# Relational graph layer: message table and per-edge gathers replaced by gathers of h, sums by (type, node) in a ring, and a transform behind a branch on TensorE

## The chip, the cores and the metric

One core of one Trainium2 chip. The metric is the device time of the whole kernel in microseconds (us), lower is better. A profile of one execution goes with each kernel. PE is TensorE, PEld its weight loads, PEq its sequencer, DVE VectorE, ACT ScalarE, POOL GpSimd, SP SyncE.

## The reference

```python
def _rgcn_layer(x, W, self_w, b, src, dst, edge_type, num_nodes):
    xW = jnp.einsum('ni,rio->rno', x, W)           # R = 8 relations, 256 x 256 each
    msg = xW[edge_type, src]                       # 320000 edges
    agg = jax.ops.segment_sum(msg, dst, num_segments=num_nodes)   # 20000 nodes
    return agg + x @ self_w + b

h = jnp.maximum(_layernorm(x, axis=-1), 0.0)
out = x + layer2(relu(layer1(h)))                  # two such layers, other weights (shortened)
```

The edges are sorted by dst, and dst is drawn so that low node numbers have many edges: the blocks of 128 nodes fill slowly at first and fast at the end.

## The kernel before

Each layer has two stages. The node phase multiplies every node by all eight matrices and writes a table of 164 MB; the edge phase gathers one row of that table per edge, 128 edges (a chunk) at a time, multiplies by a one-hot matrix and adds into an accumulator in SBUF.

```python
# node phase, per 128 nodes (cut)
for c in range(0, R * D, step):                                   # step = 512
    po = pp.tile([P, step], F32, name="po", bufs=4)
    for k in range(KD):
        nc.tensor.matmul(po[:n], lhsT=ht[:, k, :n], rhs=wf[:, k, c:c + step],
                         start=(k == 0), stop=(k == KD - 1))
    ...                                                           # copies to stage
nc.sync.dma_start(table[i * P:i * P + n].rearrange("n r o -> n (r o)"), stage[:n])

# edge phase (cut)
with tc.For_i(0, n, 1):                                           # 21 turns of 128 items a layer
    ...
    for u in range(GI):
        if u % OB == 0:
            hot = eb.tile([P, OB, P], F32, name="hot")
            nc.vector.tensor_tensor(hot, iota_f..., rel..., op=ALU.is_equal)
        msg = eb.tile([P, D], F32, name="msg", bufs=12)
        nc.gpsimd.indirect_dma_start(out=msg, ..., in_=table.rearrange("n r o -> (n r) o"), ...)
        pm = pp.tile([P, D], F32, name="pm", bufs=5)
        nc.tensor.matmul(pm, lhsT=hot[:, u % OB, :], rhs=msg, start=True, stop=True)
        a = agg[:, ds(ws[u % OB], 1), :].rearrange("p w d -> p (w d)")
        nc.vector.tensor_tensor(a, a, pm, op=ALU.add)
```

Of the kernel before, what the change touches and what calls it, by code (L numbers as in the profile page):

```python
"""Two-layer relational GNN block: out = x + rgcn2(relu(rgcn1(relu(layernorm(x))))).

Per layer:
  node phase   table[n, r] = h[n] @ W[r] for every node and relation (in DRAM), and
               agg[n] = h[n] @ self_w + b (+ x in layer 2), which stays in SBUF.
  edge phase   agg[dst] += table[src, type].  Edges are taken 128 at a time (a chunk); the
               nodes are cut into windows of 128.  One item is a (chunk, window) pair: the
               chunk's 128 messages are gathered and multiplied by the one-hot matrix of
               their places in the window.  A chunk gets an item for each window from its
               lowest to its highest dst, so any order of the edges is right; with edges  # L10
               sorted by dst there is little more than one item per chunk.
"""
# [9 lines left out]
F32 = mybir.dt.float32  # L22
I32 = mybir.dt.int32
BF16 = mybir.dt.bfloat16
AF = mybir.ActivationFunctionType
# [4 lines left out]
DVE = mybir.EngineType.DVE  # L30
P = 128
EPS = 1e-5


@with_exitstack
def gnn_kernel(ctx: ExitStack, tc: tile.TileContext, x, src, dst, etype, w1, sw1, b1, w2, sw2, b2, out):
# [4 lines left out]
    KD = D // P  # L41
    NW = (N + P - 1) // P
# [4 lines left out]
    REC = 2 * P + 1  # L47
    GI = 128
    OB = 8
    assert E % P == 0 and D % P == 0  # L50

    dram = ctx.enter_context(tc.tile_pool(name="dram", bufs=1, space=DRAM))
    table = dram.tile([N, R, D], F32, name="table")
    rec = dram.tile([C, REC], F32, name="rec")
    ends = dram.tile([1, C], F32, name="ends")

# [3 lines left out]
    iota_f = const.tile([P, P], F32, name="iota_f")  # L60
    nc.gpsimd.iota(iota_f, pattern=[[1, P]], base=0, channel_multiplier=0, allow_small_or_imprecise_dtypes=True)
    iota_p = const.tile([P, 1], F32, name="iota_p")
    nc.gpsimd.iota(iota_p, pattern=[[0, 1]], base=0, channel_multiplier=1, allow_small_or_imprecise_dtypes=True)
    eps_t = const.tile([P, 1], F32, name="eps_t")
    nc.vector.memset(eps_t, EPS)
    ngroups = const.tile([1, 1], I32, name="ngroups")

# [1 line left out]
    with tc.tile_pool(name="setup", bufs=1) as sp, tc.tile_pool(name="setup_ps", bufs=1, space=PSUM) as spp:  # L69
        src_i = sp.tile([CP, CA, P], I32, name="src_i")  # L70
        dst_i = sp.tile([CP, CA, P], I32, name="dst_i")
        typ_i = sp.tile([CP, CA, P], I32, name="typ_i")
        nc.sync.dma_start(dst_i, dst.rearrange("(p a e) -> p a e", p=CP, e=P))
        nc.scalar.dma_start(src_i, src.rearrange("(p a e) -> p a e", p=CP, e=P))
        nc.sync.dma_start(typ_i, etype.rearrange("(p a e) -> p a e", p=CP, e=P))

        rows = sp.tile([CP, CA, REC], F32, name="rows")
        nc.vector.scalar_tensor_tensor(rows[:, :, :P], src_i, float(R), typ_i, op0=ALU.mult, op1=ALU.add)
        nc.scalar.copy(rows[:, :, P:2 * P], dst_i)

        win = sp.tile([CP, 2, CA], I32, name="win")
        nc.vector.tensor_reduce(win[:, 0, :], dst_i, AX.X, ALU.min)
        nc.vector.tensor_reduce(win[:, 1, :], dst_i, AX.X, ALU.max)
        nc.vector.tensor_single_scalar(win, win, 7, ALU.arith_shift_right)
        winf = sp.tile([CP, 2, CA], F32, name="winf")
        nc.vector.tensor_copy(winf, win)
        cnt = sp.tile([CP, CA], F32, name="cnt")
        nc.vector.scalar_tensor_tensor(cnt, winf[:, 1, :], 1.0, winf[:, 0, :], op0=ALU.add, op1=ALU.subtract)
        zero = sp.tile([CP, CA], F32, name="zero")
        nc.vector.memset(zero, 0.0)  # L90
        end = sp.tile([CP, CA], F32, name="end")
        nc.vector.tensor_tensor_scan(end, cnt, zero, 0.0, ALU.add, ALU.add)
        before = sp.tile([CP, CP], F32, name="before")
        nc.vector.tensor_scalar(before, iota_f[:CP, :CP], iota_p[:CP], None, op0=ALU.is_gt)
        pre = spp.tile([CP, 1], F32, name="pre")
        nc.tensor.matmul(pre, lhsT=before, rhs=end[:, CA - 1:CA], start=True, stop=True)
        pre_s = sp.tile([CP, 1], F32, name="pre_s")
        nc.vector.tensor_copy(pre_s, pre)
        nc.vector.tensor_scalar(end, end, pre_s, None, op0=ALU.add)
        q = sp.tile([CP, CA], F32, name="q")  # L100
        nc.vector.tensor_tensor(q, end, cnt, op=ALU.subtract)
        nc.vector.tensor_tensor(rows[:, :, 2 * P], q, winf[:, 0, :], op=ALU.subtract)
        nc.sync.dma_start(rec.rearrange("(p a) r -> p a r", p=CP), rows)
        nc.scalar.dma_start(ends.rearrange("o (p a) -> (o p) a", p=CP), end)

        last = sp.tile([1, 1], F32, name="last")
        nc.sync.dma_start(last, ends[:, C - 1:C])
        last_i = sp.tile([1, 1], I32, name="last_i")
        nc.vector.tensor_scalar(last_i, last, float(GI - 1), None, op0=ALU.add)
        nc.vector.tensor_single_scalar(ngroups, last_i, 7, ALU.arith_shift_right)  # L110

    acc = ctx.enter_context(tc.tile_pool(name="acc", bufs=1))
    agg = acc.tile([P, NW, D], F32, name="agg")
    if TAIL < P:
        nc.vector.memset(agg[:, NW - 1, :], 0.0)

    def node_phase(layer, w, sw, b):
        with tc.tile_pool(name=f"na{layer}", bufs=1) as wp, tc.tile_pool(name=f"nb{layer}", bufs=2) as np_, \
                tc.tile_pool(name=f"np{layer}", bufs=2, space=PSUM) as pp:
            wt = wp.tile([P, KD, R + 1, D], F32, name="wt")  # L120
            for k in range(KD):
                nc.sync.dma_start(wt[:, k, :R, :], w[:, k * P:(k + 1) * P, :].rearrange("r i o -> i r o"))
                nc.scalar.dma_start(wt[:, k, R, :], sw[k * P:(k + 1) * P, :])
            bias = wp.tile([P, D], F32, name="bias")
            nc.scalar.dma_start(bias, b.partition_broadcast(P))
            wf = wt.rearrange("p k r o -> p k (r o)")
            for i in range(NW):
                n = P if i < NW - 1 else TAIL
                xt = np_.tile([P, D], F32, name="xt", bufs=3)
                nc.scalar.dma_start(xt[:n], x[i * P:i * P + n, :])  # L130
                if layer == 1:
                    st = np_.tile([P, 6], F32, name="st")
                    nc.vector.bn_stats(st[:n], xt[:n])  # L133
                    mv = np_.tile([P, 2], F32, name="mv")
                    nc.vector.bn_aggr(mv[:n], st[:n])
                    rs = np_.tile([P, 1], F32, name="rs")
                    nc.scalar.activation(rs[:n], mv[:n, 1:2], AF.Sqrt, bias=eps_t[:n])
                    nc.vector.reciprocal(rs[:n], rs[:n])
                    h = np_.tile([P, D], F32, name="h")
                    nc.vector.tensor_scalar(h[:n], xt[:n], mv[:n, 0:1], rs[:n], op0=ALU.subtract, op1=ALU.mult)  # L140
                    base = bias
                else:
                    h = agg[:, i, :]
                    base = np_.tile([P, D], F32, name="base")
                    nc.gpsimd.tensor_tensor(base[:n], xt[:n], bias[:n], op=ALU.add)  # L145
                pt = pp.tile([P, KD, P], F32, name="pt")
                for k in range(KD):
                    nc.tensor.transpose(pt[:, k, :n], h[:n, k * P:(k + 1) * P], ident[:n, :n])  # L148
                ht = np_.tile([P, KD, P], F32, name="ht")
                nc.scalar.activation(ht[:, :, :n], pt[:, :, :n], AF.Relu)  # L150
                stage = np_.tile([P, R * D], F32, name="stage")
                step = 512
                for c in range(0, R * D, step):
                    po = pp.tile([P, step], F32, name="po", bufs=4)
                    for k in range(KD):
                        nc.tensor.matmul(po[:n], lhsT=ht[:, k, :n], rhs=wf[:, k, c:c + step],  # L156
                                         start=(k == 0), stop=(k == KD - 1))
# [11 lines left out]
    def edge_phase(layer):  # L169
        with tc.tile_pool(name=f"ea{layer}", bufs=1) as ep, tc.tile_pool(name=f"eb{layer}", bufs=2) as eb, \  # L170
# [50 lines left out]
            with tc.For_i(0, n, 1):  # L221
                for a, bb in zip(cur, nxt):
                    nc.scalar.copy(a, bb)  # L223
# [56 lines left out]
```

## Time and profile before

| | before |
|---|---|
| time, median of 4 runs | 10729.6 us (10723.5 to 10740.6) |
| span of the profiled run | 10803.4 us |
| POOL busy / TensorE busy / VectorE busy | 52% / 66% / 36% |
| mean granted TensorE clock | 0.736 |
| node phases / edge phases | 2660 us / 8081 us |

The prediction below shows the rows of slices, the stretches, the timeline of a stretch and the groups, so they are not repeated.

### The profile page before, as it was taken

How to read it: one execution, taken by the hardware profiler on the slowest of the kernel's cores; microseconds unless marked ns; L12 is line 12 of the kernel's file. 1: busy time of each engine (PE TensorE's matmuls, PEld its weight loads, DVE VectorE, ACT ScalarE, POOL GpSimd, SP SyncE). 2: the span in 40 equal slices, each digit the busy share in tenths (PEclk: the TensorE clock that was granted, in tenths of full speed). 3: DMA queues.
4: the chain of work that ended last, by engine and by line, in shares of the span. 5: the costliest groups of instructions: out<-in, count | busy, mean ns of one | idle time of the engine just before them, and what ended most of it. 6: DMA issues, size and time to landing. Idle time of an engine off the chain costs nothing. (4 is left out here: it accounts for less than half of the span.)

```text
span 10803.4 us, 75643 instructions
## 1 busy us (share of the span) xinstructions
PE 7136.2 (66%) x17794; PEld 3836.9 (36%) x17794; DVE 3904.0 (36%) x7989; ACT 579.4 (5%) x1360; POOL 5624.2 (52%) x5585
## 2 busy tenths in 40 slices
PE   7999955556555555555599998565555555555554
PEld 3444423333333333333244444333333333333332
DVE  3333333434433433334322222433434433333333
ACT  1222200000000000000011111000000000000000
POOL 0000067666666666766600001666766666666665
PEclk9999966666666666666699999666766666666666
DMA  4333323322222223323343333223323232232324
GB/s 145 144 142 144 142 88 90 89 89 89 88 88 87 88 88 89 89 84 89 89 149 142 143 145 131 88 87 89 90 86 90 85 90 88 88 89 87 89 88 143
DMA packets 376495, 1115.33 MB, mean 103 GB/s; under 512 B 97320, under 2 KB 162184, under 8 KB 335624
## 3 DMA queue, kind: packets, MB, share of 16 engines
q0 software_dynamic: 260160, 710.78, 22.3%
q1 hardware_dynamic: 59992, 349.84, 8.7%
q10 hardware_dynamic: 56228, 53.28, 1.5%
q8 instruction: 59, 0.97, 0.0%
q14 instruction: 56, 0.46, 0.0%
HBM read 762.77 MB, written 350.74 MB: 103 GB/s over the span
## 5 line engine op out<-in xcount | busy, mean ns | idle before, releaser
L237 POOL DMA_INDIRECT msg<-table,key x5376 | 5467.3, 1017 | 2534.1 <-issue 1197.0
L241 PE MATMUL pm<-msg,hot 128*128 128x256 f32 x10752 | 4578.8, 566 | 3033.0 <-DVE agg L243 1264.6
L241 PEld LDWEIGHTS pm<-msg,hot 128*128 128x128 f32 x10752 | 2565.0, 271 | 5010.4 <-DVE agg L243 2100.4
L243 DVE TENSOR_TENSOR agg<-agg,pm 128x256 f32 x5376 | 2259.6, 420 | 2324.9 <-PE pm L241 1191.6
L156 PE MATMUL po<-wt,ht 128*128 128x512 f32 x5024 | 2227.3, 596 | 58.9 <-ACT ht L150 49.2
L230 DVE TENSOR_TENSOR hot<-iota_f,rel 128x1024 f32<-128x1024 f32 x672 | 820.8, 1227 | 2192.7 <-remote 1493.4
L156 PEld LDWEIGHTS po<-wt,ht 128*128 128x128 f32 x5024 | 940.5, 190 | 1161.3 <-issue 1039.9
L161 DVE COPY stage<-po 128x512 f32<-128x512 f32 x628 | 433.5, 691 | 1522.1 <-PE po L156 1522.1
L191 POOL DMA_INDIRECT row<-rec,ti x44 | 41.9, 952 | 1400.9 <-DVE ti L189 1388.1
L145 POOL TENSOR_TENSOR base<-xt,bias 128x256 f32<-128x256 f32 (+1 forms) x157 | 114.0, 726 | 1176.3 <-DVE agg L166 1160.5
L159 ACT COPY stage<-po 128x512 f32<-128x512 f32 x628 | 367.1, 585 | 1526.5 <-PE po L156 1485.7
L223 ACT COPY key<-key_n 128x128 int32<-128x128 int32 x42 | 12.5, 298 | 6143.7 <-PEq L221 6142.7
L164 PE MATMUL ps<-wt,ht 128*128 128x256 f32 x1256 | 323.9, 381 | 5.3 <-DMA wt<-in_L_gnn_self_w_dram 5.3
L208 PE MATMUL pt<-ident,row 128*128 128x128 f32 x44 | 19.7, 447 | 459.4 <-DMA row<-rec,ti 431.9
L164 PEld LDWEIGHTS ps<-wt,ht 128*128 128x128 f32 x1256 | 238.9, 190 | 172.2 <-issue 155.1
L208 PEld LDWEIGHTS pt<-ident,row 128*128 128x128 f32 x44 | 8.0, 182 | 489.3 <-issue 489.3
L133 DVE BATCH_NORM_STATS2 st<-xt 128x6 f32<-128x256 f32 (+1 forms) x157 | 64.7, 412 | 263.0 <-DMA xt<-in_x_dram 263.0
L187 DVE TENSOR_SCALAR_CACHE_REDUCE hit<-endb,item 128x2500 bf16<-128x2500 f32 x44 | 124.0, 2817 | 59.1 <-PEq L221 44.8
L150 ACT ACTIVATE ht<-pt 128x256 f32<-128x256 f32 x314 | 103.6, 380 | 511.3 <-PE pt L148 354.3
L198 DVE TENSOR_TENSOR wv<-item,row 128x1 f32<-128x1 f32 x44 | 7.0, 160 | 329.5 <-DMA row<-rec,ti 329.5
L214 ACT CAST win_n<-pw 1x128 int32<-1x128 f32 x44 | 11.2, 254 | 1399.6 <-remote 912.3
L166 DVE TENSOR_TENSOR agg<-ps,base 128x256 f32<-128x256 f32 (+1 forms) x157 | 66.7, 425 | 48.8 <-PE ps L164 38.1
(54 smaller groups left out, 545.9 us busy)
## 6 DMA issues: line engine op xcount, KB each, us to landing
table<-stage SPq DMA_DIRECT2D x312, 1024.0 KB, 4.1
msg<-table,key POOLq DMA_INDIRECT x5376
xt<-in_x_dram ACTq DMA_DIRECT2D x312, 128.0 KB, 3.9
out_dram<-agg SPq DMA_DIRECT2D x6, 1664.0 KB, 19.6
out_dram<-agg ACTq DMA_DIRECT2D x6, 1664.0 KB, 28.3
wt<-in_L_gnn_W_dram SPq DMA_DIRECT2D x4, 1024.0 KB, 15.4
rec<-rows SPq DMA_DIRECT2D x1, 2509.8 KB
endb<-ends SPq DMA_DIRECT2D x2, 1250.0 KB
```

The lines of the kernel that those rows point to most:

```text
L145: nc.gpsimd.tensor_tensor(base[:n], xt[:n], bias[:n], op=ALU.add)
L150: nc.scalar.activation(ht[:, :, :n], pt[:, :, :n], AF.Relu)
L156: nc.tensor.matmul(po[:n], lhsT=ht[:, k, :n], rhs=wf[:, k, c:c + step], start=(k == 0), stop=(k == KD - 1))
L159: nc.scalar.copy(stage[:n, c:c + step], po[:n])
L161: nc.vector.tensor_copy(stage[:n, c:c + step], po[:n])
L164: nc.tensor.matmul(po[:n], lhsT=ht[:, k, :n], rhs=wf[:, k, R * D:], start=(k == 0), stop=(k == KD - 1))
L166: nc.vector.tensor_tensor(agg[:n, i, :], po[:n], base[:n], op=ALU.add)
L187: nc.vector.tensor_scalar(hit, endb, item, None, op0=ALU.is_le, op1=ALU.add, accum_out=t)
L230: nc.vector.tensor_tensor(hot, iota_f[:, None, :].to_broadcast([P, OB, P]), rel[:, u:u + OB, None].to_broadcast([P, OB, P]), op=ALU.is_equal)
L237: nc.gpsimd.indirect_dma_start(out=msg, out_offset=None, in_=table.rearrange("n r o -> (n r) o"), in_offset=bass.IndirectOffsetOnAxis(ap=k ...
L241: nc.tensor.matmul(pm, lhsT=hot[:, u % OB, :], rhs=msg, start=True, stop=True)
L243: nc.vector.tensor_tensor(a, a, pm, op=ALU.add)
```

## The change

The intent: a message is h[src] times W[type], and the product can be taken after the sum. So the rows of h are gathered (2500 chunks a layer, of 2 KB rows that hold the high and the low half of h), and summed by (type, node) in a ring of four slots of 128 nodes. When a block of 128 nodes is complete, its eight sums are multiplied by the eight matrices, once. The table, the node phase and its stage are gone. Work goes in "beats" of 8 chunks, 319 a layer and all unrolled; a beat after which no block is complete has nothing to transform, and TensorE branches past the 16 products. I call a beat that runs them a real one (156 a layer) and the others empty (163). In both, two products with the weights of the node itself (the self product) follow the switch, and `leave` finishes and writes out the result of the beat before. The core of the diff, with cuts:

```diff
+        def transform(stage, ht, n=P, run=None):
+            po = pp.tile([P, D], F32, name="po", bufs=2)
+            nc.tensor.matmul(po[:n], lhsT=ones[0:1, :n], rhs=bias, start=True, stop=False)
+            def products():
+                for k in range(KD):
+                    for r in range(R):
+                        nc.tensor.matmul(po[:n], lhsT=stage[:, k * R + r, :n], rhs=wt[:, k, r, :], start=False,
+                                         stop=False)
+            if run is None:
+                products()
+            else:
+                for arm in tc.Switch({PE: run}, 2):
+                    if arm == 1:
+                        products()
+            for k in range(KD):
+                nc.tensor.matmul(po[:n], lhsT=ht[:, k, :n], rhs=wt[:, k, R, :], start=False, stop=(k == KD - 1))
+            return po
 ... 
+        for g in range(G):
 ...
+                _, pv = nc.values_load_multi_w_load_instructions(
+                    tab_s[0:1, g, 1:2], engines=(PE,), min_val=0, max_val=1,
+                    skip_runtime_bounds_check_because=in_range)
 ...
+                nc.scalar.copy(stage, ring[:, :, ds(av[0], P)])
+                nc.scalar.memzero(ring[:, :, ds(av[1], P)].bitcast(I32))
+                if g + 1 < NB:
+                    hots[g + 1] = one_hot(g + 1)
+                nc.vector.tensor_tensor(stage[:, :, :NS], stage[:, :, :NS], ring[:, :, ds(vv[BEAT], NS)], op=ALU.add)
+                nc.scalar.memzero(ring[:, :, ds(av[2], NS)].bitcast(I32))
+                ht = self_t(hl)
+                if wait is not None:
+                    leave(*wait)
+                for u in range(n):
+                    msg = pool.tile([P, HL], F32R, name="msg", bufs=18)
+                    nc.gpsimd.indirect_dma_start(out=msg.bitcast(F32), out_offset=None, in_=table, ...)
+                    pm = pp.tile([P, KD, R * NS], F32, name="pm", bufs=4)
+                    for k in range(KD):
+                        for i in range(2):
+                            nc.tensor.matmul(pm[:, k, :], lhsT=msg[:, i * D + k * P:i * D + (k + 1) * P],
+                                             rhs=hot[:, u, :], ...)
+                    a = ring[:, :, ds(vv[u], NS)]
+                    nc.vector.tensor_tensor(a, a, pm.rearrange("p k (r n) -> p (k r) n", n=NS), op=ALU.add)
+                po = transform(stage, ht, run=pv[0])
+                wait = (po, xb, P, into(sv[0]), sv[1])
```

A general path for unsorted edges lies behind a flag at the end; it does not run on these inputs.

## The prediction

> **What bounds the kernel now.** I read the row of 40 slices first, then the stretches between its steps, then the costliest groups, then the timeline inside one stretch. The page:
>
> ```profile
> PE   7999955556555555555599998565555555555554
> POOL 0000067666666666766600001666766666666665
> PEclk9999966666666666666699999666766666666666
> ```
>
> Four stretches: TensorE full (node phases), then POOL at two thirds (edge phases), twice. The stretches by time, columns as named in their head:
>
> ```profile
> core 0: us, PE busy (x) PEld busy (x) DVE busy (x) ACT busy (x) POOL busy (x), PEclk, DMA share, GB/s
> 0.00:1355.00 1355.00, 1274.47 (x3456) 629.85 (x3456) 442.03 (x1117) 284.34 (x631) 0.99 (x8) 1.00 0.39 143
> 1355.00:5395.00 4040.00, 2286.29 (x5442) 1282.30 (x5442) 1587.31 (x3196) 29.74 (x129) 2759.00 (x2710) 0.66 0.30 88
> 5395.00:6700.00 1305.00, 1270.78 (x3456) 628.66 (x3454) 285.73 (x477) 235.59 (x471) 113.95 (x157) 1.00 0.39 144
> 6700.00:10741.00 4041.00, 2304.67 (x5442) 1296.13 (x5442) 1588.98 (x3200) 29.74 (x129) 2750.23 (x2710) 0.65 0.30 88
> 10741.00:10803.00 62.00, 0.00 (x0) 0.00 (x0) 0.00 (x0) 0.00 (x0) 0.00 (x0) 0.50 1.00 330
> ```
>
> So 2660 us of node phase, 8081 of edge phase, 62 of write-out. An edge phase costs 4040/2688 = 1.50 us per item (a gather of 128 rows). No engine is full there; the timeline shows the cadence:
>
> ```profile
> 5363.95 0.95 POOL L237 DMA_INDIRECT msg<-table,key  x1 [0.31 <-issue]
> 5365.20 0.95 POOL L237 DMA_INDIRECT msg<-table,key  x1 [0.30 <-issue]
> 5366.25 1.23 DVE L230 TENSOR_TENSOR hot<-iota_f,rel 128x1024 f32<-128x1024 f32 x1 [9.37 <-remote]
> 5366.45 1.84 POOL L237 DMA_INDIRECT msg<-table,key  x1 [0.30 <-remote]
> ...
> 5388.97 3.57 DVE L243 TENSOR_TENSOR agg<-agg,pm 128x256 f32 x7 [1.63 <-PE pm L241]
> ```
>
> A gather follows the last by 0.95 + 0.30 = 1.25 us when nothing stops it: that is POOL's floor, 5376 x 1.25 = 6720 us. The other 1360 us are stalls: gathers stretched to 1.84 us beside the one-hot compare, buffer waits, and the loop's end every 128 items. Seven dependent adds took 3.57 us: 0.51 each, not the 0.42 of the groups below. These are the prices I use:
>
> ```profile
> L237 POOL DMA_INDIRECT msg<-table,key x5376 | 5467.3, 1017 | 2534.1 <-issue 1197.0
> L243 DVE TENSOR_TENSOR agg<-agg,pm 128x256 f32 x5376 | 2259.6, 420 | 2324.9 <-PE pm L241 1191.6
> L156 PE MATMUL po<-wt,ht 128*128 128x512 f32 x5024 | 2227.3, 596 | 58.9 <-ACT ht L150 49.2
> L230 DVE TENSOR_TENSOR hot<-iota_f,rel 128x1024 f32<-128x1024 f32 x672 | 820.8, 1227 | 2192.7 <-remote 1493.4
> L159 ACT COPY stage<-po 128x512 f32<-128x512 f32 x628 | 367.1, 585 | 1526.5 <-PE po L156 1485.7
> L150 ACT ACTIVATE ht<-pt 128x256 f32<-128x256 f32 x314 | 103.6, 380 | 511.3 <-PE pt L148 354.3
> ```
>
> **What the Trainium skill says.** (1) "Perfetto Trace Analysis", section "DMA Instruction — SWDGE (GPSIMD)": the recorded end is when the last DSP has written its descriptors, not when data has moved. So 0.95 us is descriptor writing for 128 rows and should not grow with the row's bytes. No run here shows another row width yet. (2) "GPSIMD Engine Reference", section "1. Specifications": its SBUF interfaces contend with VectorE instructions that have two SBUF inputs. The trace agrees: 0.95 becomes 1.84 us beside the compare, which reads two SBUF tensors. (3) "FP8 and Floating Point Precision", section "TensorE Precision Notes": true FP32 takes four passes; a reduced FP32 is truncated and read natively. The trace agrees on the first: a 128x512 entry follows the last by 0.43 us at clock 1.00 and a product is two entries, 0.86 us, four times 512/2.4 GHz. The reduced form is in no run so far. (4) "TensorE: Matmul & The Clock Gate", section "LDWEIGHTS (loading the stationary operand)": 128 columns take about 107 ns. The trace records 190 ns, hidden behind the stream.
>
> **The change, part by part.**
>
> Removed: the two node phases as stages (2660 us), the message table (two 164 MB writes), the loop with its 42 ends, the final write-out (62).
>
> Gathers: 2500 a layer instead of 2688, of 2 KB rows (high and low half of h). At 1.25 us: 3125 a layer, 6250 in all; a beat of 8 takes POOL 10.0 us. The new compare reads PSUM and one SBUF tensor, so by point 2 the 1.84 us collisions should go. Transfers: 88 GB/s took a share of 0.30, so a beat's 2.1 MB of gathers plus about 0.5 MB of rows in and out, in 11 us, is 236 GB/s, at most 0.80: hidden.
>
> TensorE per beat: 8 chunks x 4 reduced-FP32 products of 192 columns. At one pass the stream is 80 ns and the weight load 107: 0.43 us a chunk, 3.4 a beat. The self rows' transposes add 0.45. The transform is 19 true-FP32 products of 256 columns at 0.43 us = 8.2, of which 16 are branched past where no block ends. So at full clock 12.0 us a real beat, about 5 an empty one. I count beats from the inputs: 319 a layer, 156 real, 163 empty; 10 real in the first 80, 65 in the last 79. No fallback is triggered (a chunk spans at most 19 nodes, the ring's backlog is 1).
>
> VectorE per beat: an add of 384 elements is 0.51 + 128/0.96 GHz = 0.64 us, eight 5.1. The compare of 1536 is 1.23 + 512/0.96 = 1.76. The stage add 0.64, the leave 0.45. Sum 8.0 us: below POOL.
>
> ScalarE: 585 and 380 ns give 0.80 ns an element + 175 ns, so copying 2048 elements of a ring slot takes 1.8 to 1.9 us and zeroing 2048 as long; zeroing 384 0.5, two more 0.38. Sum 5.0.
>
> No sum reaches POOL's 10.0 but TensorE's in real beats. **The path**, though, is the ring: its addresses are registers, so each access must wait for the last on another engine. Per empty beat in layer 1: slot copy (1.9, after the last add), zeroing (1.8), stage add (0.7), small zeroing (0.6), transposed self rows' copy (0.35), relu of the last result (0.4), its remainder on VectorE (0.55), then eight adds (5.1) = 11.4 us. In layer 2 the last result is one VectorE add that fits beside the zeroing: 10.2. A real beat is TensorE's: after the transform come the self rows (0.45), the leave (1.5 us until the adds start), and four adds before the eighth chunk gets a PSUM buffer, about 3: 8.2 + 0.45 + 1.5 + 3 = 13.2 warm; half the real beats follow an empty one and start at the lower clock, so I take 14.0, and 13.0 in layer 2.
>
> Sum: layer 1, 163 x 11.4 + 156 x 14.0 = 1858 + 2184 = 4042. Layer 2, 163 x 10.2 + 156 x 13.0 = 1663 + 2028 = 3691. Fixed: inputs and tables 85 (before's are ready at 45); layernorm 20 tiles x 9.5 = 190, from 3.1 MB a tile at 330 GB/s, the rate of the write-out; between layers 30 for landing and weights; end 20: 325. Together 8058 of span, times 10730/10803 is 8000 us.
>
> **The rivals.** (a) POOL stays the bound: the ring's chain overlaps more than I think, or the scheduler spreads it. For: every other sum is below 10.0, and 18 message buffers let gathers run a beat ahead. Against: the copy must follow the last add, and the next adds follow the zeroing. Time: 6250 + 325 + some 300 of real beats above POOL = 6900. (b) The reduced-FP32 product costs four passes at 192 columns: a chunk then takes 4 x 192 x 4/2.4 GHz = 1.28 us, a real beat 19 us, an empty one 12: 2 x (163 x 12 + 156 x 19.5) + 325 = 10300, no gain. For: the trace has only true FP32. Against: splitting h in two halves would then make no sense. (c) POOL's cost grows with bytes: at double, 2.2 us a gather, 5000 x 2.2 = 11000, slower. Against: point 1, and the record gathers of 1028 B take 0.95 like the 1024 B ones, though that is nearly the same size. (d) The transfers of 2 KB rows become the bound, or the branches cost fetches: a share of 0.80 is near enough to full that latency could rise; 8500 to 9000.
>
> **Range and chances.** The floor by gathers alone is near 6600; my chain gives 8000; a colder TensorE or slower transfers reach 8800. Predicted 8000 us, 8 in 10 between 6900 and 8800. Faster by over 2%: 0.94 (only b and c lose the gain), within 2%: 0.03, slower: 0.03.
>
> **What would show it.** Right: one long stretch a layer in place of two, gathers at 0.95 us with POOL busy about 70% there; slot copies near 1.9 us each preceded by a wait on the ring add; VectorE's first add of a beat waiting for the small zeroing or the leave; adds 0.6 us apart; empty beats of 10 to 11.5 us, real ones of 13 to 14; TensorE's share and clock rising through each layer. Wrong: gathers well above 1 us (c); weight loads or products of pm over 0.3 us apart at full clock (b); gathers that wait for nothing, back to back at 1.25 (a); a DMA share above 0.9 or adds that wait for msg transfers (d).

## More of the kernel before

In the list of DMA queues (packets, MB, share of 16 engines' time) on the page of the kernel before:

```profile
q8 instruction: 59, 0.97, 0.0%
```

Here less than 1 MB was moved in 10.8 ms.

## The result, and the profile after

| | before | after |
|---|---|---|
| time, median of 4 runs, first measurement ("first chip") | 10729.6 us | 11479.7 us (11473.2 to 11498.0) |
| ratio, first chip | 1 | 1.070 (1.069 to 1.072) |
| time, median (7 and 4 runs), a second chip | 9919.8 us | 10692.1 us |
| ratio, second chip | 1 | 1.078 (1.076 to 1.079) |

Ratios are the mean time of one kernel's fast runs over that of the other's in the same rounds, so they are not quite the ratio of the medians; the interval is of 95%. The changed kernel is correct and 7% slower. The experiments ran on three chips (4, 11 and 1); on all three the kernel before took 9920 us, 7.5% less than in the first measurement, and on the two where the changed kernel ran it took 7% less. The record has no number for the chip of the first measurement; that it was another one is inferred from the times. I call it the first chip. The ratio hardly moves.

The page of the changed kernel on the first chip. Ahead of the numbers, the rows of 40 slices and the instruction queue:

```profile
PE   0555566666667777778865556566666777777777
...
POOL 3444444444444444443434444444444444444442
PEclk9766667777777788888876666777777778888888
...
q8 instruction: 2016, 33.03, 1.2%
```

The four stretches of before are gone; two long ones remain, as predicted. But POOL stands at four tenths where the prediction asked for about 70%, and nothing else is full either: TensorE is idle a third of the time, and the clock it is granted reads 6 to 8 tenths in all slices but the first. The instruction queue moved 33 MB where before it was 1 MB. The groups (busy us, mean ns of one | idle before them and what ended most of it):

```profile
L335 POOL DMA_INDIRECT msg<-t,key x5000 | 4727.2, 945 | 6229.2 <-PE pm L340 5020.0
L344 DVE TENSOR_TENSOR ring<-ring,pm 128x384 f32 x5000 | 2771.0, 554 | 2157.6 <-remote 950.0
L275 PE MATMUL po<-wt,stage 128*128 128x256 f32 x10048 | 2860.9, 455 | 888.4 <-issue 883.3
...
L340 PE MATMUL pm<-hot,msg 128*128 128x192 f32 x20000 | 3091.6, 316 | 21.6 <-DVE stage L326 9.6
...
L284 PE MATMUL po<-wt,ht 128*128 128x256 f32 x2560 | 998.6, 529 | 2725.6 <-ACT ring L327 1066.2
L322 ACT COPY stage<-ring 128x2048 f32 x638 | 1211.1, 1898 | 5317.7 <-issue 4300.1
...
L244 DVE TENSOR_TENSOR hot<-iota,rel 128x1536 fp32r<-128x1536 f32 x626 | 1098.7, 1755 | 1017.3 <-issue 738.4
L323 ACT ACTIVATE ring<-ring x638 | 1218.6, 1910 | 20.4
```

The unit prices of POOL, VectorE and ScalarE are as predicted: a gather 945 ns, a ring add 554 (0.65 us from one to the next), the compare 1755, the slot copy 1898, the zeroing 1910. The counts are the predicted ones too. So the time is not in what these instructions cost. It is in TensorE's, which run at a lowered clock, and between instructions, and the column of idle time says before which: of POOL's 6229 us, 5020 wait for TensorE to free message buffers, so POOL is not the cause. TensorE itself stands still before two groups, 888 us before L275 (the 16 products) and 2726 us before L284 (the self product, which follows the products or the branch). Both are the places where the switch ends. "issue" means that the engine waited for nothing that the profile shows; "ACT ring L327" is a name put on a wait with no other witness, because nothing in the self product needs the ring.

The stretches put numbers on the slices (columns as in the head line):

```profile
core 0: us, PE busy (x) PEld busy (x) DVE busy (x) ACT busy (x) POOL busy (x), PEclk, DMA share, GB/s
2000.00:3500.00 1500.00, 992.78 (x4834) 858.12 (x4835) 609.35 (x946) 428.74 (x430) 648.24 (x686) 0.76 0.50 145
4500.00:5500.00 1000.00, 791.09 (x3748) 668.20 (x3749) 384.34 (x596) 272.06 (x272) 410.30 (x435) 0.83 0.49 143
```

The DMA engines are half busy, so the transfers are not the bound. Now inside two beats, a real one and an empty one after it, from the timeline of the changed kernel on the second chip, where the pattern is cleanest (start us, us, engine, line, operation, count, idle before it):

```profile
2006.37 0.69 PE L271 MATMUL po<-bias,ones 1*128 1x256 f32 x2
...
2010.10 8.85 PE L275 MATMUL po<-wt,stage 128*128 128x256 f32 x32 [3.04 <-issue]
...
2018.79 1.03 PE L284 MATMUL po<-wt,ht 128*128 128x256 f32 x4
...
2019.46 0.74 PE L262 MATMUL pt<-ident_r,hl 128*128 128x128 f32 x4
...
2020.04 4.50 PE L340 MATMUL pm<-hot,msg 128*128 128x192 f32 x32
...
2024.47 0.69 PE L271 MATMUL po<-bias,ones 1*128 1x256 f32 x2
...
2030.38 2.07 PE L284 MATMUL po<-wt,ht 128*128 128x256 f32 x4 [5.22 <-ACT ring L323]
...
2031.89 1.31 PE L262 MATMUL pt<-ident_r,hl 128*128 128x128 f32 x4
```

In the real beat TensorE stops for 3.04 us between the bias product and the 16 products. In the empty one it stops for 5.22 us between the bias product and the self product, with nothing in between at all, and then the self product takes 2.07 us in place of 1.03, the transposes 1.31 in place of 0.74: TensorE comes back at half its clock. The branches are not counted as busy and so are in no group; they are in the trace as records of TensorE's sequencer. The same two places there, with the packets of the instruction queue that start in them (start us, us, what):

```
2006.01  3.93  COMPARE_BRANCH              real beat
2007.61  0.95    instruction queue, 16384 bytes
2010.00  0.04  BRANCH_PREFETCH_HINT
2010.09        first weight load of the 16 products
...
2024.13  0.32  COMPARE_BRANCH              empty beat
2024.51  0.04  BRANCH_PREFETCH_HINT
2025.21  0.05  EVENT_SEMAPHORE             (bias products end at 2025.16)
2025.31  1.87    instruction queue, 16384 bytes
2025.42  4.91  COMPARE_BRANCH
2027.66  1.23    instruction queue, 16384 bytes
2030.38        weight load of the self product
```

In the whole trace of the first chip TensorE has 1277 such branches, two a beat and one at the end, 3273 us together; 748 of them take over 1 us, with a median of 4.07. The others take 0.30 to 0.52, with a median of 0.41. Packets of the instruction queue overlap 745 of the 748 long ones and none of the short ones. The other four engines have 639 branches each, with medians of 33 to 41 ns. And in the empty arm the sequencer first waits on a semaphore until TensorE's matmuls are done (the EVENT_SEMAPHORE above; 326 of them, one for each empty beat), so no matmul covers the branch that follows.

### The profile page after: what moved, and what is told of

Its sections match the earlier page's. It is cut to its first block, busy times and chain, and to the rows that moved or that the text cites. A ratio compares the mean times of both kernels' runs of the same rounds, so it can differ in the third digit from the quotient of the medians.

```text
span 11471.4 us, 128792 instructions
## 1 busy us (share of the span) xinstructions
PE 7540.8 (66%) x36490; PEld 6498.0 (57%) x36490; DVE 4644.8 (40%) x7448; ACT 3191.9 (28%) x2983; POOL 4834.7 (42%) x5030
## 3 DMA queue, kind: packets, MB, share of 16 engines
q8 instruction: 2016, 33.03, 1.2%
## 5 line engine op out<-in xcount | busy, mean ns | idle before, releaser
L335 POOL DMA_INDIRECT msg<-t,key x5000 | 4727.2, 945 | 6229.2 <-PE pm L340 5020.0
L344 DVE TENSOR_TENSOR ring<-ring,pm 128x384 f32 x5000 | 2771.0, 554 | 2157.6 <-remote 950.0
L275 PE MATMUL po<-wt,stage 128*128 128x256 f32 x10048 | 2860.9, 455 | 888.4 <-issue 883.3
L275 PEld LDWEIGHTS po<-wt,stage 128*128 128x128 f32 x10048 | 2309.3, 233 | 1440.6 <-issue 1012.4
L340 PE MATMUL pm<-hot,msg 128*128 128x192 f32 x20000 | 3091.6, 316 | 21.6 <-DVE stage L326 9.6
L340 PEld LDWEIGHTS pm<-hot,msg 128*128 128x128 f32 x20000 | 2912.7, 228 | 139.8 <-DVE stage L326 9.7
L284 PE MATMUL po<-wt,ht 128*128 128x256 f32 x2560 | 998.6, 529 | 2725.6 <-ACT ring L327 1066.2
L322 ACT COPY stage<-ring 128x2048 f32 x638 | 1211.1, 1898 | 5317.7 <-issue 4300.1
L284 PEld LDWEIGHTS po<-wt,ht 128*128 128x128 f32 x2560 | 620.7, 258 | 2957.3 <-ACT ring L327 1114.3
L244 DVE TENSOR_TENSOR hot<-iota,rel 128x1536 fp32r<-128x1536 f32 x626 | 1098.7, 1755 | 1017.3 <-issue 738.4
L323 ACT ACTIVATE ring<-ring x638 | 1218.6, 1910 | 20.4
L327 ACT ACTIVATE ring<-ring x638 | 333.4, 523 | 398.9 <-DVE stage L326 369.5
```

The lines of the kernel that those rows point to most:

```text
L244: nc.vector.tensor_tensor(hot[:, :n], iota[:, None, :].to_broadcast([P, n, R * NS]), rel[:, g * BEAT:g * BEAT + n, None].to_broadcast([P, ...
L275: nc.tensor.matmul(po[:n], lhsT=stage[:, k * R + r, :n], rhs=wt[:, k, r, :], start=False, stop=False)
L284: nc.tensor.matmul(po[:n], lhsT=ht[:, k, :n], rhs=wt[:, k, R, :], start=False, stop=(k == KD - 1))
L322: nc.scalar.copy(stage, ring[:, :, ds(av[0], P)])
L323: nc.scalar.memzero(ring[:, :, ds(av[1], P)].bitcast(I32))
L327: nc.scalar.memzero(ring[:, :, ds(av[2], NS)].bitcast(I32))
```

## The experiments

The theory: it is the branch. Each switch stops TensorE for about 4 to 5 us, most probably because its code is read in anew, and lowers the clock it restarts with. The rivals: the late release of the ring adds ("remote", 950 us on the first chip), the ring's chain itself being longer than I worked out, or the cost of the 16 products at a cold clock without any fault of the branch. All ratios are to the kernel before of the same rounds.

### 1. No branch: all 16 products in every beat

```diff
-                _, pv = nc.values_load_multi_w_load_instructions(
-                    tab_s[0:1, g, 1:2], engines=(PE,), min_val=0, max_val=1,
-                    skip_runtime_bounds_check_because=in_range)
...
-                po = transform(stage, ht, run=pv[0])
+                po = transform(stage, ht)
```

The result of an empty beat is not written out in either kernel, so this one is correct. The load of the branch's register on TensorE goes with the branch; in what follows it counts as part of the switch.

> Edit: TensorE no longer branches; the 16 products run in every beat, also where no block ends. Theory A (the branch itself costs: TensorE's sequencer waits 3.5 to 4.4 us per jump for instructions, twice in an empty beat, and the last chunks' adds are released late): every beat takes 8.2 us of transform + about 5.5 of chunks, self rows and waits = about 14 us, 638 x 14 + 330 = 9260 us (8800 to 9700), and the adds of a beat follow each other without gaps. Theory B (the ring's chain of ScalarE and VectorE bounds the beats, the branch is innocent): the 326 empty beats gain products of 6.9 us on top, no less than 11480 us, about 13700. Theory C (a reduced-FP32 product of 192 columns costs four passes, 1.3 us a chunk): a beat of 10.5 + 8.2 + 2 = 20 us, about 13000 us.

Measured: correct, 8701.9 us (8695 to 8710), ratio 0.877 (0.876 to 0.879). That is below the 8800 to 9700 of theory A, which had taken 14 us a beat; theories B and C are off by thousands. Its page counts 46922 matmul records on TensorE where the changed kernel's has 36490, and yet it is faster by a fifth (experiments 5 and 6 have both on one chip). From its page:

```profile
PE   0699999999999999999999999999999999999999
...
PEclk9999999999999999999999999999999999999999
...
q8 instruction: 387, 6.34, 0.3%
```

and from its timeline:

```profile
5012.47 7.17 PE L275 MATMUL po<-wt,stage 128*128 128x256 f32 x32
...
5019.48 1.03 PE L284 MATMUL po<-wt,ht 128*128 128x256 f32 x4
...
5020.16 0.74 PE L262 MATMUL pt<-ident_r,hl 128*128 128x128 f32 x4
...
5020.74 4.03 PE L337 MATMUL pm<-hot,msg 128*128 128x192 f32 x32
```

No idle time stands on these lines. From one self product to the next it is 12.85 us (5006.63 to 5019.48), the products run at 7.17 us in place of 8.85, and TensorE is the bound, as the prediction had it for a real beat.

### 2. The branch kept, always into the products

```diff
+    tab_p = keep.tile([1, G], I32, name="tab_p")
+    nc.vector.memset(tab_p, 1)
...
-                    tab_s[0:1, g, 1:2], engines=(PE,), min_val=0, max_val=1,
+                    tab_p[0:1, g:g + 1], engines=(PE,), min_val=0, max_val=1,
```

> Edit: the branch stays, its register is 1 in every beat, so the same products run as in the run without a branch and the result is right; only the jump differs. Theory A: every beat like the real ones of the changed kernel, 18.8 us in layer 1 and 18.0 in layer 2: 638 x 18.4 + 330 = 12100 us, some 2800 us slower than without the branch. Theories B and C: the same time as without the branch within 3%.

Measured: correct, 11905.4 us, ratio 1.200 (1.198 to 1.203). It is the same arithmetic as experiment 1 on the same chip with one thing added, the switch with its register load: 3203 us for 638 beats, 5.0 us a beat (2800 were expected). The groups of the 16 products in the two kernels, this one first:

```profile
L277 PE MATMUL po<-wt,stage 128*128 128x256 f32 x20480 | 5877.5, 457 | 1967.9 <-issue 1271.5
```

```profile
L275 PE MATMUL po<-wt,stage 128*128 128x256 f32 x20480 | 4612.2, 383 | 0.0
```

Idle before them: 1968/638 = 3.1 us a beat against none. Busy: (5877.5 - 4612.2)/638 = 2.0 us a beat more for the same products at a lower clock. Together 5.1: the whole difference. So the price of a switch in a real beat is the stop and the cold restart. The rivals have no part in this difference: the ring, the adds and the products are the same in both kernels.

### 3. The branch kept, never into the products

The edit of experiment 2 with the other constant:

```diff
+    nc.vector.memset(tab_p, 0)
```

The result is wrong (no message reaches the output but in the last block).

> Edit: the register is 0 in every beat: the 16 products never run (the result is wrong on purpose). Theory A: every beat like the empty ones, 16.4 us: 638 x 16.4 + 330 = 10800 us, although TensorE has 3000 us of work less. Theory B: the chain of 11.4 and 10.2 us, about 7200 us. Theory C: 10.5 + 3 us a beat, about 9000.

Measured: 9572.5 us, ratio 0.965 (0.963 to 0.967). None of the three numbers came out. Theory A had its 16.4 us a beat from the first chip; here a beat takes 14.5. What the switch costs in it is seen with experiment 4.

This trace also bears on why a branch takes so long. The register is 0 in every beat, so TensorE goes the same way at the first branch of each switch. 220 of these 638 branches took 2.1 to 4.8 us, and a packet of the instruction queue overlaps every one of them. The other 418 took 0.29 to 0.46 us, and a packet overlaps none. The second branch, which leads out of the empty arm, took 3.3 to 5.9 us in all 638 beats, each time with a packet.

### 4. Neither branch nor products

```diff
-                po = transform(stage, ht, run=pv[0])
+                po = transform(stage, ht, skip=True)     # and transform leaves the 16 products out
```

Its output is wrong, which doesn't matter for the time.

> Edit: the 16 products and the branch are both taken out (the result is wrong on purpose): what the rest of a beat costs. Theory A: the ring's chain or POOL bounds it: 10.0 to 11.5 us a beat, 638 x 10.8 + 330 = 7200 us (6700 to 7700), 3500 us less than with a branch past the products. Theory B: as with the branch that never runs them, within 3%. Theory C: 13 us or more a beat, above 8600 us.

Measured: 7288.5 us, ratio 0.735 (0.733 to 0.736). Less some 330 us outside the beats, that is 6958/638 = 10.9 us a beat, the ring's own chain. Experiment 3 does exactly this work plus 638 branches past the products, and needs 2284 us more, 3.6 us a beat. The self product in experiment 3, then here:

```profile
L286 PE MATMUL po<-wt,ht 128*128 128x256 f32 x2560 | 1325.3, 673 | 3480.9 <-issue 2261.4
```

```profile
L286 PE MATMUL po<-wt,ht 128*128 128x256 f32 x2560 | 1119.3, 581 | 18.5 <-ACT ht L266 18.5
```

The idle time before it, 3481 us or 5.5 a beat, is more than 2284; part of it took the place of waits that TensorE has here anyway (before the chunk products it idles 941 us here and 16 in experiment 3). So the rival "the ring is slower than worked out" falls: by the spacing of the slot copies a beat takes 11.65 us in layer 1 and 10.20 in layer 2, where 11.4 and 10.2 were predicted. Theory A's total was right (6700 to 7700), its difference of 3500 to experiment 3 was not.

A beat, then, on this chip, from these four kernels:

| TensorE's part of the beat | us a beat |
|---|---|
| no products, no branch (4) | 10.9 |
| products, no branch (1) | 13.1 |
| no products, branched past (3) | 14.5 |
| products, behind a branch (2) | 18.1 |

(Each is the time less 330, over 638.) The row to look at is the third: to branch past the products costs more than to run them.

### 5 and 6. The changed kernel and the kernel without the branch, again, on one chip

Experiments 1 to 4 had no run of the changed kernel beside them, and the kernel before was 8% faster there than where the changed one had been measured. So both ran on one chip, with no edit to the first and that of experiment 1 for the second.

> The changed kernel itself again, because the chip of the first four experiments ran the kernel before in 9920 us and the chip of the first measurement in 10730. If the changed kernel is bound by TensorE's branches and not by what differs between the chips, it takes 11480 us within 2% here too, whatever the kernel before does; if it shifts with the chip as the kernel before did, about 10600.

Measured: 10692.1 us (10675 to 10700), ratio 1.078 (1.076 to 1.079). The second of the two expected outcomes: the changed kernel is faster on this chip by the same 7% as the kernel before.

> The kernel without the branch, on the same chip as the changed kernel, so that the two can be divided: 8700 us within 1%, TensorE bound at 96% busy; 0.76 of the changed kernel.

Measured: 8703.0 us (8694 to 8711), ratio 0.877 (0.876 to 0.878), and 8703/10692 = 0.814 of the changed kernel on the same chip. The 8700 came out; the expected 0.76 was missed, because it had taken the changed kernel's time from the first chip.

### 7. Fifteen products always, only the last behind the branch

If the cost were the distance of the jump, or the amount of code that is skipped, a switch round a single product should be nearly free.

```diff
             else:
+                products(range(KD * R - 1))
                 for arm in tc.Switch({PE: run}, 2):
                     if arm == 1:
-                        products()
+                        products([KD * R - 1])
```

> Edit: 15 of the 16 products always run, only the last stands behind the branch (the result stays right, since a beat that ends no block stores nothing). If a branch costs by being there (each jump makes the sequencer wait for a block of instructions and each arm ends in a join), time stays near the run with the branch taken in every beat, 11900 us (11300 to 12300), and the instruction queue moves some 30 MB. If it costs by the distance jumped over, one product is a short jump: about 8800 to 9300 us and under 12 MB of instructions.

Measured: correct, 12984.3 us, ratio 1.309 (1.303 to 1.314), the slowest kernel of all. My range for "the cost is per branch" ended at 12300 and was exceeded. Its queue and two lines of its timeline:

```profile
q8 instruction: 2137, 35.01, 1.1%
```

```profile
2028.60 6.74 PE L274 MATMUL po<-wt,stage 128*128 128x256 f32 x30
...
2040.54 2.07 PE L284 MATMUL po<-wt,ht 128*128 128x256 f32 x4 [5.20 <-issue]
```

As many blocks of instructions are read as for a branch past 16 products, and the stop in this empty beat has the same size, 5.20 us, with the same half clock after it. So the cost is not by the instructions skipped. Why it is dearer than experiment 2 is not the standstill: the idle time before the 15 products and before the self product is (120 + 2046)/638 = 3.4 us a beat, against 3.1. It is the clock after it. The stop now comes after the products, so the lowered clock falls on the self product, the transposes and the chunks: a chunk product takes 385 ns on average for 282 in experiment 2, 3994 us together for 2651. The branches over 1 us are more too, 953 for 639: the 312 real beats now have a long one after their product as well (3.1 us in the median; in experiment 2 the same branch took 0.41). Where the compiler laid the arms is not on record, so it stays open why these take long here.

### 8. No branch, and the 16 products in the reduced FP32

If the transform is cheap there is nothing to branch past. The stage and the weights are rounded to the reduced form that the chunk products use already, without a split into two halves.

```diff
+        wr = big.tile([P, KD, R, D], F32R, name="wr")
+        nc.scalar.copy(wr, wt[:, :, :R, :])
...
-    nc.tensor.matmul(po[:n], lhsT=stage[:, k * R + r, :n], rhs=wt[:, k, r, :], start=False, stop=False)
+    nc.tensor.matmul(po[:n], lhsT=stage[:, k * R + r, :n], rhs=wr[:, k, r, :], start=False, stop=False)
...
-                stage = pool.tile([P, KD * R, P], F32, name="stage")
+                stage = pool.tile([P, KD * R, P], F32R, name="stage")
```

and the call of `transform` without `run`, as in experiment 1; where VectorE adds into `stage` it is read as plain FP32.

> Edit: no branch, and the 16 products read the stage and the weights in reduced FP32 (each rounded when copied); it may miss the tolerance. If TensorE's 13 us a beat are what bounds the kernel without a branch, a product falls from 0.43 to about 0.12 us, TensorE to 8 us a beat, and the ring's chain or POOL takes over as in the run without products: 7300 us (7000 to 7700). If something else bounds it (ring chain already 13 us), 8700 us.

Measured: correct, 7475.6 us (7472 to 7479), within the expected 7000 to 7700, ratio 0.754 (0.752 to 0.755); 7476/8703 = 0.859 of experiment 6 on the same chip. It beats both kernels. By the comparison with the reference the loss of digits is within what is allowed; by how much is not in the result. From its page:

```profile
PE 54%; ACT 22%; DVE 15%; issue 4%; DMA 2%; DVEq 1%; ACTq 1%; POOL 1%; POOLq 0%
```

The chain that ended last now runs over TensorE, ScalarE and VectorE: (7476 - 330)/638 = 11.2 us a beat against the 10.9 of the kernel with no products at all. The transform is nearly hidden, in every beat, real or empty.

### 9 and 10. The kernel before and the changed kernel, once more, for the difference between chips

No edit to either.

> The kernel before itself, for its trace on whichever chip this is. It took 10730 us where it was first measured and 9920 us on the chip of the experiments. If the 8% lie in late semaphore releases between VectorE and the others, a chip on which it takes about 9920 us shows its idle time on VectorE put down to remote releases well under the 1975 us of the first trace; if they lie in the gathers or the TensorE clock, those means differ instead (945 ns a gather, or the granted clock).

Measured: 9921.1 us. The prediction quotes these two groups from the first chip; here they read

```profile
L243 DVE TENSOR_TENSOR agg<-agg,pm 128x256 f32 x5376 | 2260.2, 420 | 1764.8 <-PE pm L241 1453.4
...
L230 DVE TENSOR_TENSOR hot<-iota_f,rel 128x1024 f32<-128x1024 f32 x672 | 819.3, 1224 | 1861.3 <-PE pm L241 1861.3
```

On the first chip 1493 us of the compare's idle time were put down to "remote", a release that the profile could not name; here none, on any engine. VectorE's durations are the same; a gather took 981 ns for 1017, and the one-hot products took longer, 649 ns for 566, at a granted clock of 0.676 for 0.736, and the kernel was faster all the same.

> The changed kernel again, beside the kernel before on the same chip. If the difference between chips moves both alike, the ratio is 1.07 to 1.08 whichever chip it is. If the branch's cost depended on the chip, the ratio would move while the kernel before stays.

Measured: 10655.4 us, 1.074 times the 9920 of the kernel before beside it. In the changed kernel the same thing shows: the ring adds had 950 us of "remote" on the first chip; on the second

```profile
L344 DVE TENSOR_TENSOR ring<-ring,pm 128x384 f32 x5000 | 2770.9, 554 | 887.6 <-PE pm L340 533.0
```

So the late releases stand in the first chip's traces alone, and in those of both kernels; the ratio is nearly the same without them (1.078 and 1.074 for 1.070). That they make up the 7 to 8%, and why they come there, is not settled by any run here.

## Why the prediction was wrong

The prediction was 8000 us, from 6900 to 8800, with 0.94 on faster. It was 11480, or 10692 on a chip where the kernel before is faster as well. By its own steps:

- **Gathers at 0.95 us whatever the row's width: right.** 945 ns for 2 KB rows, and 1.25 us from one to the next where nothing stops them. Rival (c) falls. That they no longer collide with the compare is right too: none of the 5000 took over 1.27 us on the second chip, where 2.02 was the longest before.
- **The reduced FP32 in one pass: right.** 32 entries of a beat at full clock took 4.03 us in experiment 1, 0.50 a chunk, where 0.43 was worked out; four passes would have been 1.28. Rival (b) falls.
- **VectorE and ScalarE: right.** Adds 0.65 apart (8 in 5.17 us in experiment 1), compare 1.755, copy and zeroing 1.90 and 1.91.
- **The empty beat without TensorE in the way, 11.4 and 10.2: right.** Experiment 4 gives 11.65 and 10.20.
- **The real beat, 14.0 and 13.0: right without the branch.** Experiment 1 gives 13.4 and 12.8.
- **The failed step: "8.2, of which 16 are branched past where no block ends".** The branch appears in the sum as products saved, and with no cost of its own; rival (d) gave "the branches cost fetches" half a clause and at most 9000 us for it and the transfers together, and the signs of being wrong had none for it. Measured, a switch costs a real beat 5.0 us (3.1 of standstill and 2.0 of colder clock), and an empty beat 3.6 over the ring's chain. By the spacing of the slot copies in the trace of the second chip, empty beats took 14.4 us in layer 1 and 14.5 in layer 2, real ones 18.4 and 17.8. In the prediction's sum: 163 x 14.4 + 163 x 14.5 + 156 x 18.4 + 156 x 17.8 + 325 = 4711 + 5647 + 325 = 10683, and the measured span is 10689. Against the predicted 8058, the empty beats add 4711 - 3521 = 1190 us and the real ones 5647 - 4212 = 1435. That is the whole miss on this chip. The first chip adds another 783 us (11471.4 - 10688.5 of span), which the kernel before pays as well.
- **The range.** With a free branch the measured beats would give 326 x 10.9 + 312 x 13.1 + 325 = 7966 us, an estimate from experiments 1 and 4; the prediction of 8000 was a good one of that kernel, which does not exist. That it would have come so near is in part luck: it was made for the first chip, where both kernels take some 7% longer. The chances left no room for it because the branch had been put among the rivals as a matter of transfers, not as a wait on the engine that sets a real beat's end.
- **The DMA share** was to be at most 0.80 and was 0.50, since the same bytes took longer. Rival (d) as far as it concerns transfers falls. **Rival (a)**, POOL as the bound, falls with POOL at 42%.

What the prediction could have seen: the trace of before did not show this price, for TensorE's branch at the end of a turn took 0.22 us there and read no instructions. But the change has 638 switches in unrolled code. The Trainium skill, in "Runtime: NRT & Kernel Launch", section "Instruction fetch mechanics", warns that a taken branch whose target is outside the current window of pages forces a fetch of the target page before execution goes on. The prediction read other pages. The traces agree that pages are fetched: the blocks in the instruction queue are of 16 KB, and there are 2016 packets in the changed kernel against 387 without the switch. The page's reason fits what the traces show: in the kernels with a switch nearly every branch over 1 us has a read beside it and no short one has, also where TensorE goes the same way each time (experiment 3), and the loop's branch in the kernel before, with no read, took 0.22 us. That the switch is the cause is shown by experiments 1 to 4; that the sequencer waits for the read rests on these pairs, and no run changed the read alone.

Where the gain went, in one line: on one chip, the new algorithm by itself takes the kernel from 9920 to 8703 us, and the switch that was to save another 700 of it (326 empty beats at 13.1 - 10.9) costs 1989.

## What to carry to other kernels

Price a branch on an engine before counting what it skips: here a switch on TensorE cost 3.6 to 5 us a beat, the lower clock after it included, where running the 16 products behind it added 2.2 (13.1 - 10.9). Prefer to run the work always and make it cheap, as the reduced-FP32 transform did (7476 us), or to decide with data, as this kernel does elsewhere by a dummy address and a conditional write (their price was not measured). When no engine is full and the durations don't account for the time, look at the records that are not counted as busy, and at the instruction queue's bytes.

## What the Trainium skill lacked or had wrong

- "Advanced Engine Details and Errata", section "Control Flow Timing", gives about 108 ns for a compare-and-branch and 51 ns for a plain one, for no engine in particular. Here, in the changed kernel, a compare-and-branch took 33 to 41 ns (medians) on VectorE, ScalarE, GpSimd and SyncE; on TensorE 0.41 us (median of the 529 short ones) and 4.07 us (median of the 748 over 1 us), and 0.22 us in the loop of the kernel before.
- "Runtime: NRT & Kernel Launch", section "Instruction fetch mechanics", names the stall but gives it no size, and ties it to a target outside the current window. The switch round one product (experiment 7) stopped TensorE for 5.2 us in an empty beat and had 2137 instruction packets, no fewer than the one round 16 (2016); where the targets lay is not on record.
- No page that I read has the wait at the head of an empty arm until TensorE's matmuls are done (an EVENT_SEMAPHORE of the switch's line, 326 in the changed kernel), which kept the second branch from overlapping the 15 products ahead of it in experiment 7.
- "TensorE: Matmul & The Clock Gate", section "What's actually happening", has the array at half clock after an idle window of about 3.4 us. After a stop of 5.2 us the trace agrees (self product 2.07 us for 1.03); after one of 3.04 us, somewhat less than that figure, the trace grants 0.5 for 3.41 us from 0.3 us after the products began, and they took 8.85 us for 7.17. No page that I read counts this in the price of a branch.
- No page that I read says that the same kernel can differ so between occasions, most probably chips: it took 10730 us in the first measurement and 9920 on three chips later, with 1493 us of unnamed late releases before one group in the first trace and none in the later one.
